# A cross-attention kernel: x added to the output by an adding transfer, a tile of its own for the returning values, and new orders of the work

## The chip, the cores and the metric

The kernel runs on one core of one Trainium2 chip. The core has TensorE (PE in the profile, with its weight loads as PEld), VectorE (DVE), ScalarE (ACT), GpSimd (POOL) and SyncE (SP), on-chip memory (SBUF), eight banks of accumulator memory in front of TensorE (PSUM) and 16 DMA engines. The metric is the device time of one execution in microseconds (us); the time before is the median of three executions. All times below are microseconds unless ns is written.

## The reference

For each of 32 batches there are x and y (the context), both 256 channels by 1024 positions in float32. What is computed, cut to what matters:

```python
x_q = einsum('oc,bcn->bno', w_qk, y)
x_k = einsum('oc,bcn->bon', w_qk, x)
x_v = einsum('oc,bcn->bon', w_v, x) + b_v
energy = einsum('bnc,bcm->bnm', x_q, x_k)              # 1024 x 1024 a batch
attention = softmax(energy, axis=-1)
attention = attention / (1e-07 + attention.sum(axis=1, keepdims=True))
x_r = einsum('bcn,bnm->bcm', x_v, attention)
out = x + relu(einsum('oc,bcn->bon', w_t, x - x_r) + b_t)
```

## The kernel before

**What TensorE multiplies.** A number in float32 is carried as forms of TensorE's faster type: a rounded high form, a rest form (what the rounding lost) and a low form (the high one scaled down by 4096, plus the rest). Each product is then three products with the three forms. The weights are prepared once: gw (w_qk with itself, so that keys of x meet raw y), vw (w_t with w_v, so that the values already carry the last projection) and tw (w_t). After that, each batch is 22 blocks of 12 matrix products, of 512 columns each:

- k0, k1: keys (`keys`, line 431), gw with x's forms; the result becomes gf's three forms by one ScalarE and two VectorE instructions.
- v0, v1: values (`values`, line 436), one for each half of the positions. They come out with channels on partitions and are needed with positions there: VectorE transposes 32 x 32 blocks into `turned`, four transfers on SP's queue put that into the DRAM tile `blocks`, and one more transfer brings it back in the new order. The first half comes back into the tile `yr`, the second into `turned`. ScalarE and GpSimd make uf's forms of it. In the tokens below the first half is v0 for the next batch (computed ahead), the second V1 in its own batch.
- W0, W1: w_t times x (`straight`, line 486), put into `xe` by ScalarE.
- E0 to E7: energies of 128 positions (`energy`, line 494), gf with y's forms yf. Then VectorE takes the minimum of each row, ScalarE the exponential with the row's sum, VectorE the reciprocal; VectorE adds the normalized rows to the column sums (`acc`), ScalarE makes ef's high form, VectorE its rest form, both on halves of 512 columns, ScalarE the scaled high form and GpSimd adds the rest to it.
- A0 to A7: attention times values (`attention`, line 549), ef with uf, summed in PSUM over the eight.

S are the column sums' last steps (`sums`, line 563) and O the finish of a batch (`finish`, line 589): for each half of the channels VectorE scales the attention's result into `z`, GpSimd adds xe, ScalarE takes the ReLU, SP's queue loads x again into the tile `xo`, GpSimd adds it, and SP's queue stores z to the output. X (`load_x`, line 372) loads the next batch's x and makes its three forms; Y2 and Y3 (`load_y`, line 340) do so for the two halves of the next batch's y. There the third form is -high by ScalarE, to which an adding transfer on GpSimd's queue adds y from DRAM; the low form is the scaled high, to which a second adding transfer, waiting for the first, adds the third. The first piece of the first half of batch 0 is done by GpSimd instead.

**PSUM.** The eight banks are four pairs. Pairs 2 and 3 take the attention's sums, and before A0 also the blocks marked ^ in the tokens (`high_pair`); pairs 0 and 1 take all other blocks in turn (`next_pair`). A block must wait until the pair's last user has been read.

**What sets the order.** The program first lists all operations: SET_UP, then for each batch the tokens of FIRST (batch 0), STEADY (batches 1 to 29), BEFORE (batch 30) or LAST (lines 167 to 181). TensorE's order is that of the tokens. For the other queues (VectorE, ScalarE, GpSimd, SP) the class `Plan` plays the list through with a price for each operation (lines 240 to 267: columns by a rate, plus a constant, plus a lag; a landing time for each transfer) and takes, on each engine, the ready operation that is due first. The due times are worked out from the end. What comes out is one fixed order for each queue, tied by the class `InOrder` (line 221); its call is line 231, so nearly every instruction in the profile bears L231, and groups are told apart by their tiles. On the chip each queue runs in that order and waits at an instruction whose input is not there.

## Time and profile before

| | |
|---|---|
| median of three executions | 1881.93 us (1878.26 to 1883.33) |
| the profiled execution: time, span from first to last instruction | 1882.61 us, 1880.7 us |
| granted TensorE clock, mean | 0.998 |
| busy: PE, DVE, ACT, POOL | 99%, 79%, 79%, 82% |
| DMA: bytes, mean rate | 301.88 MB, 161 GB/s |
| DMA queues, share of the 16 engines: hardware (SP's), software (GpSimd's) | 34.4%, 31.0% |

A row of a timeline holds the start and the time taken, the engine, the line, the operation, what it writes and reads, how many instructions were merged, and in brackets how long the engine had been idle before it and what ended that. A row of a group holds the total busy time, the mean of one in ns, and the idle time before the group's instructions. A row of a window holds its ends and length, then busy time and count for PE, PEld, DVE, ACT and POOL, the granted clock, the share of time that the DMA engines were busy and their rate. A row of waits names who waited for whom: total, times, longest. A row of a transfer ends with its size and the median time from issue to landing. Matrix products overlap, so a block's length is read from the start of one block to the start of the next.

### The profile page before, as it was taken

How to read it: one execution, taken by the hardware profiler on the slowest of the kernel's cores; microseconds unless marked ns; L12 is line 12 of the kernel's file. 1: busy time of each engine (PE TensorE's matmuls, PEld its weight loads, DVE VectorE, ACT ScalarE, POOL GpSimd, SP SyncE). 2: the span in 40 equal slices, each digit the busy share in tenths (PEclk: the TensorE clock that was granted, in tenths of full speed). 3: DMA queues.
4: the chain of work that ended last, by engine and by line, in shares of the span. 5: the costliest groups of instructions: out<-in, count | busy, mean ns of one | idle time of the engine just before them, and what ended most of it. 6: DMA issues, size and time to landing. Idle time of an engine off the chain costs nothing.

```text
span 1880.7 us, 24352 instructions
## 1 busy us (share of the span) xinstructions
PE 1855.6 (99%) x8494; PEld 1597.4 (85%) x8494; DVE 1493.0 (79%) x2106; ACT 1484.8 (79%) x1936; POOL 1541.4 (82%) x773
## 2 busy tenths in 40 slices
PE   8999999999999999999999999999999999999998
PEld 7888888888888888888888888888888888888887
DVE  6787777887778878878777787777887877877878
ACT  6788777897777987778877789777797777887775
POOL 4788888888788888788888888888888788888777
PEclk9999999999999999999999999999999999999999
DMA  6666766667667667666676666666767666667652
GB/s 187 137 154 169 178 157 157 162 163 178 160 154 170 154 183 173 152 153 162 167 180 157 157 160 165 175 160 152 174 152 184 169 154 151 170 165 177 150 119 79
DMA packets 128651, 301.88 MB, mean 161 GB/s; under 512 B 12688, under 2 KB 47120, under 8 KB 128528
## 3 DMA queue, kind: packets, MB, share of 16 engines
q1 hardware_dynamic: 92272, 200.45, 34.4%
q0 software_dynamic: 35680, 99.10, 31.0%
q8 instruction: 66, 1.08, 0.2%
q10 hardware_dynamic: 576, 0.79, 0.1%
q14 instruction: 57, 0.47, 0.1%
HBM read 167.38 MB, written 67.11 MB: 125 GB/s over the span
## 4 chain that ended last, share of the span: by engine, by line
PE 33%; ACT 28%; DVE 14%; DMA 11%; issue 8%; POOL 4%; SPq 1%; DVEq 0%; POOLq 0%; ACTq 0%
PE banks L231 33%; ACT ef L231 10%; DMA blocks<-turned 6%; ACT banks L231 5%; DVE ef L231 5%; ACT xf L231 5%; DMA yr<-blocks 4%; DVE acc L231 4%; ACT xe L231 3%; ACT uf L231 3%; POOL ef L231 2%; DVE small L231 2%; ACT z L231 1%; SPq L231 1%; DVE parts L231 1%
## 5 line engine op out<-in xcount | busy, mean ns | idle before, releaser
L231 PE MATMUL banks<-gf,yf 128*128 128x512 f32 x3072 | 705.5, 381 | 8.5 <-DMA yf<-yf 2.8
L231 POOL TENSOR_TENSOR ef<-ef 128x1024 fp32r<-128x1024 f32 x256 | 640.5, 2516 | 79.8 <-DVE acc L231 35.4
L231 PE MATMUL banks<-ef,uf 128*128 128x512 f32 x3072 | 694.7, 379 | 1.1 <-POOL ef L231 0.6
L231 PEld LDWEIGHTS banks<-gf,yf 128*128 128x128 f32 x3072 | 576.2, 189 | 107.5 <-DVE ef L231 24.9
L231 PEld LDWEIGHTS banks<-ef,uf 128*128 128x128 f32 x3072 | 580.2, 189 | 85.1 <-POOL ef L231 1.4
L231 DVE TENSOR_REDUCE small<-banks 128x1 f32<-128x1024 f32 x256 | 312.5, 1221 | 174.1 <-PE banks L231 174.1
L231 DVE SCALAR_TENSOR_TENSOR ef<-banks,small,ef 128x512 fp32r<-128x512 f32 x512 | 366.5, 742 | 48.5 <-ACT ef L231 47.6
L231 ACT ACTIVATE ef<-banks,small 128x512 fp32r<-128x512 f32 x512 | 335.5, 706 | 4.1 <-DVE acc L231 0.6
L231 DVE SCALAR_TENSOR_TENSOR acc<-banks,small,acc 128x512 f32<-128x512 f32 x448 | 319.6, 743 | 5.7
L231 ACT ACTIVATE banks<-banks,small 128x1024 f32<-128x1024 f32 x256 | 281.8, 1101 | 23.2 <-DVE small L231 23.0
L231 ACT ACTIVATE ef<-ef 128x1024 fp32r<-128x1024 f32 x256 | 276.7, 1081 | 1.2
L231 ACT ACTIVATE gf<-banks 128x1024 fp32r<-128x1024 f32 x64 | 65.4, 1023 | 261.7 <-PE banks L231 259.8
L231 POOL TENSOR_TENSOR z<-z,xe 128x1024 f32<-128x1024 f32 (+1 forms) x64 | 149.1, 2345 | 68.2 <-DVE z L231 65.7
L231 POOL TENSOR_TENSOR uf<-yr,uf 128x1024 fp32r<-128x1024 f32 x64 | 152.2, 2377 | 57.4 <-ACT uf L231 57.1
L231 PE MATMUL banks<-xf,vw 128*128 128x512 f32 x768 | 183.4, 383 | 7.5 <-DVE ef L231 6.7
L231 PE MATMUL banks<-xf,gw 128*128 128x512 f32 x768 | 177.3, 380 | 1.1 <-DVE xf L231 0.7
L231 PE MATMUL banks<-xf,tw 128*128 128x512 f32 x774 | 176.5, 378 | 0.9 <-DVE banks L231 0.9
L231 PEld LDWEIGHTS banks<-xf,vw 128*128 128x128 f32 x768 | 142.6, 189 | 38.2 <-DVE ef L231 19.2
L231 PEld LDWEIGHTS banks<-xf,gw 128*128 128x128 f32 x768 | 144.7, 189 | 23.5 <-ACT acc L231 1.1
L231 PEld LDWEIGHTS banks<-xf,tw 128*128 128x128 f32 x774 | 145.4, 189 | 22.1 <-DVE banks L231 1.3
L231 POOL TENSOR_TENSOR uf<-turned,uf 128x1024 fp32r<-128x1024 f32 x64 | 154.9, 2420 | 8.5 <-ACT uf L231 6.2
L231 POOL TENSOR_TENSOR xf<-xr,xf 128x1024 fp32r<-128x1024 f32 x62 | 149.3, 2429 | 1.0 <-ACT xf L231 1.0
(68 smaller groups left out, 1633.8 us busy)
## 6 DMA issues: line engine op xcount, KB each, us to landing
yr<-in_ctx_dram SPq DMA_DIRECT2D x64, 512.0 KB, 4.3
blocks<-turned SPq DMA_DIRECT2D x256, 128.0 KB, 3.2
yf<-in_ctx_dram POOLq DMA_DIRECT2D x63, 512.0 KB, 6.1
yf<-yf POOLq DMA_DIRECT2D x63, 512.0 KB, 7.4
xo<-in_x_dram SPq DMA_DIRECT2D x62, 512.0 KB, 4.4
xr<-in_x_dram SPq DMA_DIRECT2D x62, 512.0 KB, 4.8
xf<-xf POOLq DMA_DIRECT2D x62, 512.0 KB, 6.7
out_dram<-z SPq DMA_DIRECT2D x62, 512.0 KB, 4.1
```

Of the source, the lines that this page charges most:

```text
L231: self.last = getattr(self.engine, name)(*args, **kwargs)
```

## The change

- `finish`: the load of x into `xo` and GpSimd's addition go; in their place an adding transfer on GpSimd's queue adds x from DRAM to z after the ReLU. The tile `xo` goes.
- `load_y`: for all pieces but the first of all, the third form is now y minus the high form, by GpSimd from `yr`; ScalarE's -high and the adding transfer from DRAM go. The second adding transfer (third to low) stays.
- `values`: the first half comes back to a new tile `vb` and no longer to `yr`.
- `energy`: the column sums and the high and rest forms are written as three functions that can each work on halves or on the whole; SUMS, HIGHS and RESTS are 2, halves as before. They are listed sums, high forms, rest forms, and no longer half by half.
- All five token strings are new, and so are several of the planner's prices and landing times.

```diff
+SUMS, HIGHS, RESTS = 2, 2, 2
+LAND_Y, LAND_X, LAND_BLOCKS, LAND_BACK, LAND_LOW, LAND_Z = 7.6, 5.6, 3.4, 3.5, 7.0, 7.1
 SET_UP = (
-    "z z x0 z z z z G H fH00 x1 fH01 T fR01 fL00 y fR00 fL01 Q fR11 fH10 fR10 fL10 b fH11 fL11"
+    "z G z z z z x0 z fH00 y T fR01 fH01 x1 H fL01 Q fL00 fR10 fH10 fR00 fL10 fL11 b fR11 fH11"
 )
 FIRST = (
-    "V0^ W0^ W1^ E0 E1^ V1^ E2 E3 A0 A1 E4 X Y2 E5 A2 A3 E6 E7 A4 Y3 A5 v0 k0 S A6 A7 k1 O"
+    "V0^ W0^ E0 W1^ E1^ E2 V1^ E3 X A0 E4 Y2 A1 E5 A2 A3 E6 E7 A4 A5 k1 v0 Y3 A6 S A7 O k0"
 )
 STEADY = (
-    "W0^ E0^ E1 E2 W1^ V1^ E3 Y2 A0 E4 A1 E5 A2 X E6 A3 E7 Y3 S A4 A5 v0 k1 A6 A7 k0 O"
+    "W0 E0^ E1 E2 V1^ W1^ E3 A0 E4 A1 E5 X A2 A3 E6 E7 A4 A5 Y2 k0 v0 A6 S A7 O k1 Y3"
 )
 BEFORE = (
-    "V1^ E0 W0^ E1 W1^ X E2 A0 E3 A1 E4 A2 E5 A3 E6 E7 Y2 A4 Y3 A5 v0 k0 k1 A6 S A7 O"
+    "V1^ E0 W0 E1^ W1^ E2 E3 X A0 A1 E4 A2 E5 A3 E6 E7 A4 A5 Y2 Y3 v0 k1 A6 k0 S A7 O"
 )
 LAST = (
-    "E0 E1^ V1^ E2 E3 A0 A1 E4 E5 A2 A3 E6 R1 E7 A4 A5 W0 A6 a0 S a1 D1 F1 G0"
+    "E0 R1 E1^ V1^ E2 E3 A0 A1 E4 A2 E5 A3 E6 E7 A4 A5 W0 A6 S a0 a1 D1 F1 G0"
 )
...
-        plan.add("act", columns / 1200 + 0.1 + more, 0.09, reads, writes, trace)
+        plan.add("act", columns / 1200 + 0.13 + more, 0.1, reads, writes, trace)
...
-        plan.add("dve", columns / 960 + 0.16, 0.0, reads, writes, trace, early=early)
+        busy = columns / 960 + (0.08 if columns > MB else 0.13)
+        plan.add("dve", busy, 0.08, reads, writes, trace, early=early)
...
-        busy = columns * 2.25 / 1024 + 0.12
-        plan.add("pool", busy, 0.0, reads, writes, trace, port=busy)
+        busy = columns * 2.25 / 1024 + 0.07
+        plan.add("pool", busy, 0.08, reads, writes, trace, port=busy)
...
-    xo = one.tile([P, N], F32, name="xo")
+    vb = one.tile([P, N], F32, name="vb")
...
-            on_act(columns, nh, nr, lambda: act.mul(third, value(high), -1.0))
-            by_pool(7.2, nr, nr, lambda: accumulate(third, from_[:, :, at]))
+            on_pool(
+                columns, ["yr"] + nh, nr,
+                lambda: pool.tensor_tensor(third, r[:, :, at], value(high), ALU.subtract),
+            )
...
-        plan.add("sync", 2.4, 3.0 if b else 5.0, ["turned"], ["blocks"], out_of)
-        back, name = (turned, "turned") if q else (flat(yr), "yr")
-        by_sync(4.5, ["blocks"], [name], lambda: sync.dma_start(back, blocks))
+        plan.add("sync", 1.75, LAND_BLOCKS if b else 5.0, ["turned"], ["blocks"], out_of)
+        back, name = (turned, "turned") if q else (vb, "vb")
+        by_sync(LAND_BACK, ["blocks"], [name], lambda: sync.dma_start(back, blocks))
...
-        for h in range(MH):
-            halves(h)
+        each, whole = [[h] for h in range(MH)], [list(range(MH))]
+        for make, pieces in ((column_sums, SUMS), (high_form, HIGHS), (rest_form, RESTS)):
+            for hs in each if pieces == MH else whole:
+                make(hs)
...
-                by_sync(5.2, ["bias"], ["xo"], lambda: sync.dma_start(xo, x[b, ts(c, P)]))
-                on_pool(
-                    N, [f"z{c}", "xo"], [f"z{c}"],
-                    lambda: pool.tensor_tensor(z[:, c], z[:, c], xo, ALU.add),
-                )
+                by_pool(LAND_Z, [f"z{c}"], [f"z{c}"], lambda: accumulate(z[:, c], x[b, ts(c, P)]))
```

The other landing times become LAND_Y (y, 5.8 before), LAND_X (x, 5.0), LAND_LOW (the transfers into low forms, 5.8 for y and 8.2 for x).

More of the change, by code (lines that the diff above doesn't have):

```diff
@@ L376, in of @@
                 raw = [f"xr{k}{h}" for h in range(MH)]
[L377 to L378 removed]
+                by_sync(LAND_X, ["yr"] if b == 1 else [], raw, lambda: sync.dma_start(xr[:, k], x[b, ts(k, P)]))
+                on_act(
+                    N, raw, x_names(HIGH, k), lambda: act.copy(parted(xf[:, HIGH, k]), in_turn(xr[:, k])), more=0.47
+                )
                 on_pool(
@@ L517, in energy, with part @@
             N, at + [nm[0]], at + [nm[1]],
-            lambda: act.activation(p, p, AF.Exp, bias=low, scale=-1.0, accum_out=rs), more=0.193,
+            lambda: act.activation(p, p, AF.Exp, bias=low, scale=-1.0, accum_out=rs), more=0.1,
         )
         dve_small(0.18, [nm[1]], [nm[2]], lambda: dve.reciprocal(ri, rs))
-        def halves(h):
-            ph, a, turns = both[:, h], acc[:, ts(h, MB)], in_turn(both[:, h])
-            to = {j: parted_half(f[:, j], h) for j in (HIGH, REST)}
-            high, rest = names[HIGH][h], names[REST][h]
+        def part(t, hs):
+            return t[:, hs[0] * MB : (hs[-1] + 1) * MB]
@@ L526, in halves, with column_sums @@
+        def column_sums(hs):
+            ph, a = part(p, hs), part(acc, hs)
+            banks_, sums_ = [at[h] for h in hs], [f"acc{h}" for h in hs]
             if n == 0:
-                on_dve(MB, [at[h], nm[2]], [f"acc{h}"], lambda: dve.tensor_scalar(a, ph, ri, None, ALU.mult))
+                on_dve(
+                    MB * len(hs), banks_ + [nm[2]], sums_,
+                    lambda: dve.tensor_scalar(a, ph, ri, None, ALU.mult),
+                )
             else:
                 on_dve(
-                    MB, [at[h], nm[2], f"acc{h}"], [f"acc{h}"],
+                    MB * len(hs), banks_ + [nm[2]] + sums_, sums_,
@@ L531, in halves, with turned_to, high_form @@
                     lambda: dve.scalar_tensor_tensor(a, ph, ri, a, ALU.mult, ALU.add),
                 )
-            on_act(MB, [at[h], nm[2]], [high], lambda: act.mul(to[HIGH], turns, ri))
+        def turned_to(j, hs):
+            return parted(f[:, j])[:, :, hs[0] * MB // 2 : (hs[-1] + 1) * MB // 2]
+        def high_form(hs):
+            turns = in_turn(part(p, hs))
+            on_act(
+                MB * len(hs), [at[h] for h in hs] + [nm[2]], [names[HIGH][h] for h in hs],
+                lambda: act.mul(turned_to(HIGH, hs), turns, ri),
+            )
@@ L534, in halves, with rest_form @@
+        def rest_form(hs):
+            turns = in_turn(part(p, hs))
             on_dve(
-                MB, [at[h], nm[2], high], [rest],
+                MB * len(hs), [at[h] for h in hs] + [nm[2]] + [names[HIGH][h] for h in hs],
+                [names[REST][h] for h in hs],
                 lambda: dve.scalar_tensor_tensor(
-                    to[REST], turns, ri, value(to[HIGH]), ALU.mult, ALU.subtract
+                    turned_to(REST, hs), turns, ri, value(turned_to(HIGH, hs)), ALU.mult, ALU.subtract
```

10 lines of the change are left out of this document (4 added, 6 removed).

## The prediction

> **What bounds the kernel now.** The page's first part comes first: TensorE (PE) is busy 99%, the others 79 to 82%.
>
> ```profile
> PE 1855.6 (99%) x8494; PEld 1597.4 (85%) x8494; DVE 1493.0 (79%) x2106; ACT 1484.8 (79%) x1936; POOL 1541.4 (82%) x773
> ```
>
> So only time in which PE waits can be won. The timeline of PE shows where. One batch, from its E0 to the next:
>
> ```profile
> 899.46 7.93 PE L231 MATMUL banks<-gf,yf 128*128 128x512 f32 x36
> 907.23 2.75 PE L231 MATMUL banks<-xf,tw 128*128 128x512 f32 x12
> 909.82 1.46 PE L231 MATMUL banks<-xf,vw 128*128 128x512 f32 x6
> 911.94 1.56 PE L231 MATMUL banks<-xf,vw 128*128 128x512 f32 x6 [0.66 <-DVE ef L231]
> ...
> 918.54 3.15 PE L231 MATMUL banks<-gf,yf 128*128 128x512 f32 x12
> 921.53 2.75 PE L231 MATMUL banks<-ef,uf 128*128 128x512 f32 x12
> ...
> 944.84 2.75 PE L231 MATMUL banks<-xf,gw 128*128 128x512 f32 x12
> ...
> 957.79 4.48 PE L231 MATMUL banks<-gf,yf 128*128 128x512 f32 x20
> ```
>
> Read the starts. A block of 12 products takes 907.23 to 909.82, 2.59 us, and a batch has 22 blocks, 56.98 us. This batch takes 957.79 - 899.46 = 58.33, so it lost 1.35: 0.93 in the middle of V1 (six products there took 2.12 in place of 1.30), some 0.4 in E4 (918.54 to 921.53 is 2.99), and little else. Over the 27 periods from the third batch's E0 to the thirtieth's, the stage's window and its waits say:
>
> ```profile
> 147.48:1708.89 1561.41, 1553.22 (x7130) 1340.44 (x7128) 1248.27 (x1756) 1249.42 (x1620) 1305.12 (x649) 1.00 0.68 164
> ...
> ACT uf L231 <- DMA yr<-blocks: 62.8, 27, 3.5
> ```
>
> 1561.41 - 27 x 56.98 = 22.9 us lost, 0.85 a period, at a full clock. ScalarE waits 2.3 us in each period for the values' return from DRAM. That return decides the loss, as three batches show (E0's start, the cast that ends the wait for the return, the next E0; for the middle one 899.46 and 957.79 stand above):
>
> ```profile
> 87.43 7.93 PE L231 MATMUL banks<-gf,yf 128*128 128x512 f32 x36
> 92.00 1.05 ACT L231 CAST uf<-yr 128x1024 fp32r<-128x1024 f32 x1 [2.31 <-DMA yr<-blocks]
> 147.48 7.93 PE L231 MATMUL banks<-gf,yf 128*128 128x512 f32 x36
> ...
> 901.93 1.05 ACT L231 CAST uf<-yr 128x1024 fp32r<-128x1024 f32 x1 [2.90 <-DMA yr<-blocks]
> 904.84 1.08 ACT L231 ACTIVATE banks<-banks,small 128x1024 f32<-128x1024 f32 x1
> ...
> 959.23 1.04 ACT L231 CAST uf<-yr 128x1024 fp32r<-128x1024 f32 x1 [1.87 <-DMA yr<-blocks]
> 1015.35 4.91 PE L231 MATMUL banks<-gf,yf 128*128 128x512 f32 x22
> ```
>
> Return after E0's start: 4.57, 2.47, 1.44 us. Lost in that period: 3.07 (60.05), 1.35, 0.58 (57.56). So 0.8 us is lost for each us that the return is later. The way: E0's exponential (904.84) stands behind the cast in ScalarE's queue, E0's forms come late, and V1 waits for E0's bank.
>
> The opening has its own loss:
>
> ```profile
> 17.87 2.75 PE L231 MATMUL banks<-xf,vw 128*128 128x512 f32 x12
> ...
> 33.41 1.03 PE L231 MATMUL banks<-gf,yf 128*128 128x512 f32 x4
> 37.27 6.27 PE L231 MATMUL banks<-gf,yf 128*128 128x512 f32 x20 [2.84 <-DMA yf<-yf]
> 43.38 5.34 PE L231 MATMUL banks<-ef,uf 128*128 128x512 f32 x24
> ...
> 37.20:41.50 4.30, 4.23 (x12) 3.40 (x13) 2.92 (x4) 2.70 (x3) 3.13 (x2) 0.60 1.00 214
> ```
>
> E2 and E3 of batch 0 took 9.97 for 5.18: 3.0 idle for y's adding transfer, and then 1.8 because the clock was granted at 0.60. From 17.87 to 87.43 lie 24 blocks, 62.2 us, in 69.56: 7.4 lost, 4.8 of it here.
>
> By the Trainium skill ("TensorE: Matmul & The Clock Gate", HAM oscillation) the clock halves after gaps over some 3.4 us; here some 3.0 were enough. By that rule or by the row, the 1.8 go as soon as this gap is shorter; the sum below has them gone in either case.
>
> **The change, part by part.** These groups and transfers carry the costs:
>
> ```profile
> L231 POOL TENSOR_TENSOR z<-z,xo 128x1024 f32<-128x1024 f32 x62 | 147.1, 2373 | 0.0
> L231 ACT ACTIVATE yf<-yf 128x1024 fp32r<-128x1024 f32 x126 | 140.1, 1112 | 0.0
> L231 POOL DMA_DIRECT2D yf<-in_ctx_dram x64 | 78.6, 1234 | 30.3 <-DVE ef L231 25.7 <-ACT yf L231 4.6
> ...
> yf<-in_ctx_dram POOLq DMA_DIRECT2D x63, 512.0 KB, 6.1
> yf<-yf POOLq DMA_DIRECT2D x63, 512.0 KB, 7.4
> ```
>
> *x added by a transfer.* 62 GpSimd adds (147 us) and 62 loads on SP's queue go, and 62 adding transfers come. Nothing shows their price; the nearest is y's adding transfer from DRAM, 1.23 us on GpSimd and 6.1 to land. The output leaves some 4 us later, and nobody waits: z is written again a batch later. GpSimd now stands at such a transfer until the ReLU is done, with uf's and the first ef's sums behind it; at worst that delays A0.
>
> *y's third form on GpSimd.* 63 multiplications go from ScalarE (63 x 1.112 = 70 us, 2.2 a batch), and 64 transfers from GpSimd (79); 63 subtractions come, of the removed add's size (2.37, together 149). GpSimd: -147 + 76 - 79 + 149 = -1 us of 1541. That is no gain and no loss; ScalarE alone is relieved, and y waits for one landing where it waited for two.
>
> *Sums and forms in new functions.* With the three settings at 2 they are the same instructions on the same halves: nothing.
>
> *A tile of its own (vb), the orders, the planner's prices.* SP's queue and yr are freed. In the new order v0 is followed by A6, A7, k1, W0 and then E0: four blocks, 10.36 us, where it had five. How long the return takes:
>
> ```profile
> 945.94 1.25 DVE L231 STREAM_TRANSPOSE turned<-banks 128x1024 f32<-128x1024 f32 x1
> 947.22 2.44 SPq L231 DMA_DIRECT2D blocks<-turned  x4
> 955.57 0.34 SPq L231 DMA_DIRECT2D yr<-blocks  x1
> ...
> 915.89 1.77 SPq L231 DMA_DIRECT2D blocks<-turned  x4
> 920.62 0.34 SPq L231 DMA_DIRECT2D turned<-blocks  x1
> ...
> 915.90:920.60 4.70, 4.57 (x21) 3.69 (x21) 3.30 (x5) 4.70 (x6) 4.70 (x3) 1.00 0.49 123
> 947.20:955.60 8.40, 8.40 (x40) 7.37 (x39) 6.04 (x5) 1.23 (x2) 4.06 (x4) 1.00 1.05 215
> ```
>
> v0 ended at 944.84. The transpose came 1.10 later, behind the column sums' small steps, which now have 2.6 us more to be over (I take 0.2). Then 1.28 to the first piece's issue, 8.35 to the return's issue while the DMA engines are full (1.05), against 4.73 for v1 where they are half free (0.49), and 3.66 to the cast. In the new order the cast comes 0.2 + 1.28 + L + 3.66 - 10.36 = L - 5.22 after E0's start. L lies between 4.73 and 8.35. Two of the four y transfers of a batch are gone beside it and x's two adding ones start later, so I take the middle, 6.54: 1.3 us after E0's start. By the line above that loses 0.55 a period in place of 0.85: 27 x 0.3 = **-8.0**. Ends: L of 4.73 and E4's wait gone too, -22.9; L of 8.35, +3.1 us, 1.9 a period, +28. That W1 and V1 change places alters no distance: W1 now waits for E0's bank three blocks after it.
>
> *Set-up.* G's products are put ahead of five of the ten fillers.
>
> ```profile
> 1.06 4.63 PE L231 MATMUL banks<-few 128*128 128x128 f32 x20 [1.06 <-DVE few L231]
> 5.48 2.63 PE L231 MATMUL banks<-z 128*128 128x256 f32 x8
> ```
>
> Half of the fillers are 2.2 us, so G can start by up to that much earlier, if its weights are there; but two more steps (4 products, 0.86) now follow the last low piece, which VectorE makes late. Between -2.2 and +0.9; I take less than the middle, as the weights' landing is not told: **-0.4**.
>
> *Batch 0.* The second piece's third form is one subtraction now, not a transfer.
>
> ```profile
> 19.30 1.72 POOL L231 TENSOR_TENSOR yf<-yf 128x512 fp32r<-128x512 f32 x1
> 24.18 1.22 DVE L231 SCALAR_TENSOR_TENSOR gf<-banks,gf 128x1024 fp32r<-128x1024 f32 x1
> 26.37 1.69 POOL L231 DMA_DIRECT2D yf<-yf  x1
> ```
>
> GpSimd is free at 21.0, a half subtraction later (1.2) the low transfer starts at some 22.3 instead of 26.37, and lands after 7.4 (its row) or 10.9 (37.27 - 26.37): 29.7 to 33.2. E2 now comes after five blocks, at 30.4, and needs it 0.9 later: 0 to 1.9 lost. E0 moves up to 22.7 (two blocks after 17.5) and needs gf's last form, ready at 25.4, or 24.2 if the values' transpose gives way, from 24.4 on: 0 to 1.0 lost. Together some 1.3, against 4.8. But PE then reaches the rest earlier than ScalarE and VectorE have moved, so part comes back: **-3.5**, ends -7.4 and +1. The first steady period falls from 3.07 to some 1.2: **-1.9** (-3.1 to +1).
>
> *The end.* From 1708.89 on I can price no wait of the new order: **-0.5**, ends -4 and +3.
>
> The sum is -0.4 - 3.5 - 1.9 - 8.0 - 0.5 = -14.3. The profiled execution took 1882.6 (span 1880.7), 0.7 above the median of 1881.93: 1868.3, and about **1868** as a median.
>
> **The rivals.** Told from no change here is 0.3%, 5.6 us: 1876.3 to 1887.6.
>
> 1. *Only the opening gains.* The return comes as late as before, the steady loss stays 0.85. For it: one block less of distance. Against: less traffic, a freer ScalarE. 1882.6 - 6.3 = 1876.
> 2. *The return comes later (slower).* The blocks land as slowly as now (L 8.35), as the four-block distance is not made good; x's adding transfers crowd the way back. 1882.6 - 6.3 + 28 = 1905; it decides from a return 2.1 us after E0's start on, where the opening's gain is eaten. For it: the full DMA engines in the window. Against: two transfers fewer in it, and xe and the ReLU can run ahead of the late cast.
>
>    The Trainium skill ("DMA: Bandwidth & Descriptors", Issuing engines are not separate DMA queues) speaks for this rival: transfers from all queues run on the same 16 engines and interleave, so moving x's to GpSimd's queue frees none. The two windows agree.
> 3. *Nearly all waits go.* The return comes before E0 (L below 5.2) and E4's bank is in time: 1882.6 - 22.9 - 6.3 = 1853.
> 4. *Nothing moves.* What the opening wins, ScalarE and VectorE give back in batch 0, and the orders trade one wait for another: 1882.
>
> **How the numbers follow.** The forecast 0.45, rivals 0.18, 0.17, 0.12, 0.08. Low 1850 takes in the third. High 1892 is the second with L of 7.7 (2.5 after E0, 1.43 a period, +15.7 with the opening's -6.3); what lies above is some one in ten. Faster: most of the forecast, half of the first rival, the third: 0.64. Slower: nearly all of the second and a little of the fourth: 0.18. Same: 0.18.
>
> **What would show it.** Right: E0-to-E0 periods of 57.4 to 57.6; the cast from vb within 1.5 us of E0's start; no half clock after 30 us; ScalarE 70 us less busy, GpSimd within 20 of 1541. Wrong: periods of 58 and over with ScalarE waiting over 2.5 us for vb; PE waiting for POOL's ef before A0, which would mean that GpSimd stands at x's transfer; a new wait at k0 or v0, which now follow E6 and E7 by three blocks each; or a wait for y in E2 longer than 2 us.

## The result, and the profile after

| | before | after |
|---|---|---|
| median of four executions each | 1880.1 us (1877.52 to 1883.33) | 1847.99 us (1847.77 to 1848.07) |
| ratio after / before, 95% interval | | 0.9828 (0.981 to 0.9846) |
| span of the profiled execution | 1880.7 us | 1846.1 us |
| bytes moved | 301.88 MB | 268.58 MB |

The change made the kernel 1.7% faster, more than twice the 13.6 us that were forecast, and 2 us below the low end of the range. The instructions of the kernel after bear L233, since two lines were added above the call.

The first and the fourth part of the page of the kernel after (busy time by engine; the chain that ended last, by engine):

```profile
PE 1835.8 (99%) x8494; PEld 1603.5 (87%) x8494; DVE 1478.3 (80%) x2106; ACT 1462.4 (79%) x1872; POOL 1523.1 (83%) x773
...
PE 95%; DVE 2%; DMA 2%; SPq 0%; issue 0%; ACT 0%; POOL 0%; DVEq 0%; ACTq 0%
```

PE's share reads 99% as before, and says nothing of the gain. The chain does: PE now makes 95% of it. In the kernel before, the same row gave PE 33%, ACT 28%, DVE 14% and DMA 11%, so the path went in and out of TensorE all the time. Now the end of the program hangs on TensorE alone, nearly everywhere.

One steady batch of the kernel after, in PE's timeline, up to A1 (the next E0 starts at 993.18):

```profile
936.21 7.93 PE L233 MATMUL banks<-gf,yf 128*128 128x512 f32 x36
943.98 2.75 PE L233 MATMUL banks<-xf,vw 128*128 128x512 f32 x12
946.57 2.75 PE L233 MATMUL banks<-xf,tw 128*128 128x512 f32 x12
949.15 2.75 PE L233 MATMUL banks<-gf,yf 128*128 128x512 f32 x12
951.74 2.75 PE L233 MATMUL banks<-ef,uf 128*128 128x512 f32 x12
954.33 2.75 PE L233 MATMUL banks<-gf,yf 128*128 128x512 f32 x12
956.92 2.75 PE L233 MATMUL banks<-ef,uf 128*128 128x512 f32 x12
```

Every start is 2.59 behind the last one: V1 runs through (before, 0.93 was lost in its middle), and E4 to A1 is 2.59 (before, 2.99). The period is 56.97, the bare 22 blocks. The window over the same 27 periods as in the prediction, and ScalarE's row among the waits:

```profile
138.21:1677.08 1538.87, 1538.87 (x7129) 1346.93 (x7128) 1235.29 (x1756) 1233.00 (x1566) 1288.33 (x649) 1.00 0.59 148
```

```profile
ACT uf L233 <- DMA vb<-blocks: 1.9, 2, 1.0
```

1538.87 - 27 x 56.98 = 0.41 us lost, against 22.95. ScalarE waited for the return twice in the whole run. SP's and ScalarE's timelines around one return (batch with E0 at 1107.15) show how early it is:

```profile
1098.89 1.79 SPq L233 DMA_DIRECT2D blocks<-turned  x4
1102.59 0.34 SPq L233 DMA_DIRECT2D vb<-blocks  x1
```

```profile
1108.36 1.03 ACT L233 CAST uf<-vb 128x1024 fp32r<-128x1024 f32 x1
1111.19 1.09 ACT L233 ACTIVATE banks<-banks,small 128x1024 f32<-128x1024 f32 x1 [0.85 <-DVE small L233]
```

The way through DRAM (first transfer of the blocks to the issue of the return, L in the prediction) took 3.70, where 8.35 was read before and 6.54 was forecast. The cast from vb has no wait in brackets: it starts 1.21 after E0, as in all steady batches, because xe's instruction stands ahead of it in ScalarE's queue. E0's exponential now waits for VectorE's minimum of the row, not for the cast.

The opening of the kernel after, in PE's timeline (16.62 is the first product of the values):

```profile
16.62 2.75 PE L233 MATMUL banks<-xf,vw 128*128 128x512 f32 x12
...
21.92 3.21 PE L233 MATMUL banks<-gf,yf 128*128 128x512 f32 x12
24.96 2.75 PE L233 MATMUL banks<-xf,tw 128*128 128x512 f32 x12
...
37.91 0.46 PE L233 MATMUL banks<-ef,uf 128*128 128x512 f32 x1
39.56 2.88 PE L233 MATMUL banks<-ef,uf 128*128 128x512 f32 x11 [1.19 <-DVE ef L233]
42.28 2.86 PE L233 MATMUL banks<-gf,yf 128*128 128x512 f32 x12
```

The wait for y's adding transfer is gone. What is left is 0.45 in E0 (24.96 - 21.92 = 3.04 for 2.59) and 1.78 in A0 (42.28 - 37.91 = 4.37), whose first ef comes late. The granted clock from 16.62 to the next batch's E0 at 81.23 is 1.00. So the 34.5 us of the two spans divide thus:

| stretch | lost before | lost after | gain | forecast |
|---|---|---|---|---|
| set-up, to the values' first product | 17.87 | 16.62 | 1.25 | 0.4 |
| batch 0 | 7.41 | 2.45 | 4.96 | 3.5 |
| first steady period | 3.07 | 0.00 | 3.07 | 1.9 |
| 27 steady periods | 22.95 | 0.41 | 22.54 | 8.0 |
| last three batches, and what follows the last product | 10.1 | 7.4 | 2.7 | 0.5 |

(The set-up's two entries are times, not losses.) Two thirds of the gain, and 14.5 of the 20.2 us that the forecast missed, lie in the steady periods. There the experiments were made.

### The profile page after: what moved, and what is told of

Its sections match the earlier page's. It is cut to its first block, busy times and chain, and to the rows that moved or that the text cites. A ratio compares the mean times of both kernels' runs of the same rounds, so it can differ in the third digit from the quotient of the medians.

```text
span 1846.1 us, 24208 instructions
## 1 busy us (share of the span) xinstructions
PE 1835.8 (99%) x8494; PEld 1603.5 (87%) x8494; DVE 1478.3 (80%) x2106; ACT 1462.4 (79%) x1872; POOL 1523.1 (83%) x773
## 2 busy tenths in 40 slices
DMA packets 111242, 268.58 MB, mean 145 GB/s; under 512 B 11664, under 2 KB 45840, under 8 KB 111120
## 3 DMA queue, kind: packets, MB, share of 16 engines
q8 instruction: 66, 1.08, 0.2%
## 4 chain that ended last, share of the span: by engine, by line
PE 95%; DVE 2%; DMA 2%; SPq 0%; issue 0%; ACT 0%; POOL 0%; DVEq 0%; ACTq 0%
PE banks L233 95%; DMA blocks<-turned 1%; DMA vb<-blocks 1%; DVE ef L233 0%; DVE acc L233 0%; SPq L233 0%; DMA z<-in_L_xattn_w_t_dram 0%; DVE small L233 0%; DMA turned<-blocks 0%; DVE parts L233 0%; DVE turned L233 0%; DVE z L233 0%; DVE rc L233 0%; POOL uf L233 0%; ACT banks L233 0%
## 5 line engine op out<-in xcount | busy, mean ns | idle before, releaser
L233 POOL TENSOR_TENSOR ef<-ef 128x1024 fp32r<-128x1024 f32 x256 | 624.4, 2460 | 93.2 <-ACT ef L233 64.9
L233 PE MATMUL banks<-gf,yf 128*128 128x512 f32 x3072 | 691.0, 379 | 1.7 <-DVE ef L233 1.6
L233 PE MATMUL banks<-ef,uf 128*128 128x512 f32 x3072 | 690.1, 379 | 1.2 <-DVE ef L233 1.2
L233 PEld LDWEIGHTS banks<-gf,yf 128*128 128x128 f32 x3072 | 579.8, 189 | 86.7 <-DVE ef L233 3.7
L233 PEld LDWEIGHTS banks<-ef,uf 128*128 128x128 f32 x3072 | 580.2, 189 | 85.0 <-DVE ef L233 1.9
L233 DVE TENSOR_REDUCE small<-banks 128x1 f32<-128x1024 f32 x256 | 312.5, 1221 | 155.7 <-PE banks L233 155.6
L233 DVE SCALAR_TENSOR_TENSOR ef<-banks,small,ef 128x512 fp32r<-128x512 f32 x512 | 371.6, 743 | 46.0 <-ACT ef L233 45.3
L233 ACT ACTIVATE ef<-banks,small 128x512 fp32r<-128x512 f32 x512 | 333.6, 685 | 48.7 <-DVE acc L233 44.7
L233 DVE SCALAR_TENSOR_TENSOR acc<-banks,small,acc 128x512 f32<-128x512 f32 x448 | 323.0, 746 | 5.8
L233 ACT ACTIVATE banks<-banks,small 128x1024 f32<-128x1024 f32 x256 | 278.7, 1089 | 52.1 <-DVE small L233 49.5
L233 ACT ACTIVATE ef<-ef 128x1024 fp32r<-128x1024 f32 x256 | 267.8, 1060 | 4.1
L233 POOL TENSOR_TENSOR z<-z,xe 128x1024 f32<-128x1024 f32 (+1 forms) x64 | 158.1, 2473 | 98.2 <-DVE z L233 96.6
L233 ACT ACTIVATE gf<-banks 128x1024 fp32r<-128x1024 f32 x64 | 65.4, 1023 | 217.7 <-PE banks L233 217.6
L233 POOL TENSOR_TENSOR xf<-xr,xf 128x1024 fp32r<-128x1024 f32 x62 | 150.3, 2424 | 73.9 <-ACT xf L233 73.9
L233 POOL TENSOR_TENSOR uf<-vb,uf 128x1024 fp32r<-128x1024 f32 x64 | 156.1, 2439 | 30.3 <-ACT uf L233 30.3
L233 PE MATMUL banks<-xf,tw 128*128 128x512 f32 x774 | 176.3, 378 | 1.1 <-DVE banks L233 1.1
L233 PE MATMUL banks<-xf,gw 128*128 128x512 f32 x768 | 177.1, 380 | 0.0
L233 PE MATMUL banks<-xf,vw 128*128 128x512 f32 x768 | 176.2, 379 | 0.0
L233 POOL TENSOR_TENSOR yf<-yr,yf 128x1024 fp32r<-128x1024 f32 (+1 forms) x65 | 164.2, 2527 | 5.4 <-ACT yf L233 5.4
L233 PEld LDWEIGHTS banks<-xf,tw 128*128 128x128 f32 x774 | 145.4, 189 | 21.9 <-DVE banks L233 1.5
L233 PEld LDWEIGHTS banks<-xf,vw 128*128 128x128 f32 x768 | 145.2, 189 | 20.6
L233 PEld LDWEIGHTS banks<-xf,gw 128*128 128x128 f32 x768 | 145.0, 189 | 20.5
```

Source lines behind the costliest of these rows:

```text
L233: self.last = getattr(self.engine, name)(*args, **kwargs)
```

## The experiments

**How they are read.** Each kernel's steady loss is the time from the third batch's E0 to the thirtieth's, less 27 x 56.98, from its own trace. The ratio is to runs of the kernel before on the same chip. The ratio's interval reaches 0.1 to 0.5% to either side, so a difference of a few us between two rows rests on the steady loss, not on the ratio. The rows come from several chips, so close medians are compared by their ratios.

| kernel | median us | ratio (95%) | steady loss, a period |
|---|---|---|---|
| before | 1880 | 1 | 0.85 |
| work of after, orders and prices of before | 1871.41 | 0.9964 (0.9948 to 0.998) | 0.62 |
| orders and prices of after, work of before | 2372.42 | 1.2623 (1.257 to 1.2675) | 17.6 |
| before, with only y's subtraction on GpSimd | 1872.61 | 0.996 (0.9944 to 0.9975) | 0.72 |
| after, y's third form by transfer as before | 2082.25 | 1.1079 (1.102 to 1.1137) | 7.4 |
| after, first half back to yr | 2174.67 | 1.1571 (1.1527 to 1.1614) | 11.0 |
| after, x added by GpSimd | 1846.68 | 0.9825 (0.9796 to 0.9853) | 0.00 |
| after, tokens of before | 1855.37 | 0.9871 (0.9842 to 0.99) | 0.15 |
| after, prices of before | 1867.83 | 0.9933 (0.9911 to 0.9956) | 0.31 |
| work of after + VectorE's prices | 1866.57 | 0.9915 (0.9882 to 0.9948) | 0.58 |
| work of after + GpSimd's prices, landing times | 1872.27 | 0.9942 (0.9918 to 0.9967) | 0.76 |
| work of after + ScalarE's prices | 1859.33 | 0.9877 (0.9841 to 0.9912) | 0.15 |
| work of after + price of the cast of x | 1859.81 | 0.9887 (0.9844 to 0.9929) | 0.26 |
| work of after + ScalarE's other prices | 1860.22 | 0.9889 (0.9845 to 0.9933) | 0.31 |
| before + price of the cast of x | 1875.86 | 0.9974 (0.9963 to 0.9985) | 0.60 |
| after, STEADY's tokens for batch 30 | 1848.08 | 0.9817 (0.9782 to 0.9851) | 0.015 |
| after, x added by GpSimd, STEADY's tokens for batch 30 | 1847.55 | 0.9821 (0.9779 to 0.9863) | 0.01 |
| after | 1847.99 | 0.9828 (0.981 to 0.9846) | 0.015 |

### Work and orders apart

The first question was whether the steady gain comes from the instructions and transfers of the change (its "work") or from its orders, that is its token strings and prices.

The work alone: after, with the five token strings and all prices of before.

```diff
 STEADY = (
-    "W0 E0^ E1 E2 V1^ W1^ E3 A0 E4 A1 E5 X A2 A3 E6 E7 A4 A5 Y2 k0 v0 A6 S A7 O k1 Y3"
+    "W0^ E0^ E1 E2 W1^ V1^ E3 Y2 A0 E4 A1 E5 A2 X E6 A3 E7 Y3 S A4 A5 v0 k1 A6 A7 k0 O"
...
-        plan.add("act", columns / 1200 + 0.13 + more, 0.1, reads, writes, trace)
+        plan.add("act", columns / 1200 + 0.1 + more, 0.09, reads, writes, trace)
```

> The work of after (x by an adding transfer, y's third form on GpSimd, vb) with the token strings and the planner's prices and landing times of before. Traffic theory: the return is issued some 4 us after the first blocks transfer, ScalarE waits for it less than 0.3 a period, V1's wait of some 0.45 a period goes and only E4's 0.4 stays; 1862 to 1870. Order theory: the loss stays at 0.7 to 0.9 a period, 1876 to 1882.

Orders and prices alone: after, with y's third form, the return to yr and x's addition as before.

```diff
-        back, name = (turned, "turned") if q else (vb, "vb")
+        back, name = (turned, "turned") if q else (flat(yr), "yr")
...
-                by_pool(LAND_Z, [f"z{c}"], [f"z{c}"], lambda: accumulate(z[:, c], x[b, ts(c, P)]))
+                by_sync(5.2, ["bias"], ["xo"], lambda: sync.dma_start(xo, x[b, ts(c, P)]))
```

> The work of before (x added by GpSimd from xo, y's third form by ScalarE and a transfer from DRAM, the values back in yr) with the token strings and the planner's prices of after. Traffic theory (the steady loss hangs on how late the values' return is, and that on y's transfers from DRAM beside it): the return is issued 6 to 8 us after the first blocks transfer, and the steady loss stays at 0.6 to 1.5 us a period; 1870 to 1900. Order theory (the orders and prices alone take the waits away): at most 0.2 a period, 1850 to 1860.

The orders alone are 26% slower. The waits of that kernel:

```profile
PE banks L233 <- DMA yf<-in_ctx_dram: 250.6, 30, 9.1
...
PE banks L233 <- DMA yf<-yf: 112.1, 30, 5.1
```

The new strings put Y2 and Y3 late in the batch, shortly before the y they make is needed. With two adding transfers behind each other TensorE then waits up to 9.1 us, and the granted clock is 0.90 on the mean. The tile yr, which y and the returning values share here as before, has a part in it: in one batch (return issued at 971.70) y's next load into yr is issued only 11.0 later. Neither theory had this. So the orders can only be had with the new work.

The work alone gains 0.4% and keeps 0.62 of the 0.85; its 1871.41 lies between the two theories. SP's and PE's timelines of one batch of it:

```profile
939.35 1.79 SPq L233 DMA_DIRECT2D blocks<-turned  x4
944.58 0.34 SPq L233 DMA_DIRECT2D vb<-blocks  x1
```

```profile
949.73 7.93 PE L233 MATMUL banks<-gf,yf 128*128 128x512 f32 x36
...
960.09 2.91 PE L233 MATMUL banks<-xf,vw 128*128 128x512 f32 x12
962.84 2.77 PE L233 MATMUL banks<-gf,yf 128*128 128x512 f32 x12
...
968.04 3.15 PE L233 MATMUL banks<-gf,yf 128*128 128x512 f32 x12
971.02 2.75 PE L233 MATMUL banks<-ef,uf 128*128 128x512 f32 x12
```

The return is issued 5.15 ahead of E0, and nothing waits for it. Still V1 takes 2.75 from start to start and E4 2.98: 0.16 and 0.39, together with 0.02 in E3 the 0.58 that nearly every batch of this kernel loses. In this kernel, too, the cast starts 1.21 after E0, the earliest that xe ahead of it allows. So the prediction's third batch, with its cast at 1.44, stood at the foot of the line, and the 0.58 that it lost is the same 0.58.

The trace of before says so too, if all of its 27 steady batches are read and not three. None loses less than 0.58. Six lose 0.58 or 0.59, with casts from 1.04 to 1.67 after E0 (a seventh, at 1.66, loses the same in V1, E3 and E4, and 0.20 more in A2 and E6). From there the loss rises about one for one: 0.76 at 1.89, 0.93 at 2.05, 1.35 at 2.48, 1.93 at 3.05. The slope of 0.8 was a chord across this bend. Of the 22.95 us, 27 x 0.58 = 15.7 are there however early the return comes, and 7.3 come with its lateness. **The 0.58 was never the return's.**

### The parts of the work

Before, with nothing but y's subtraction:

```diff
-            on_act(columns, nh, nr, lambda: act.mul(third, value(high), -1.0))
-            by_pool(7.2, nr, nr, lambda: accumulate(third, from_[:, :, at]))
+            on_pool(
+                columns, ["yr"] + nh, nr,
+                lambda: pool.tensor_tensor(third, r[:, :, at], value(high), ALU.subtract),
+            )
```

> Before with one edit: y's third form is y minus the high form by GpSimd (no multiplication on ScalarE, no transfer of y from DRAM). Traffic theory: this part alone brings the return forward: 4 to 5.5 us from the first blocks transfer to the return's issue (8.35 before), ScalarE's wait for yr from 2.3 a period to under 0.5, the loss from 0.85 to 0.6 a period, the opening 3 us better; 1868 to 1874. If the own tile or x's transfer is what matters: 0.8 to 0.9 a period, 1876 to 1882. As GpSimd gets 73 us more to do here (86% busy), a third way is that it holds up ef's sums: over 1882.

The steady loss falls to 0.72, and the opening gains most: the third batch's E0 comes at 139.44 (147.48 before, 138.22 after). SP's timeline and the waits:

```profile
936.62 1.78 SPq L231 DMA_DIRECT2D blocks<-turned  x4
944.13 0.34 SPq L231 DMA_DIRECT2D yr<-blocks  x1
```

```profile
ACT uf L231 <- DMA yr<-blocks: 8.1, 9, 4.0
```

The way through DRAM is still 7.51, so that y's two transfers fewer do not shorten it much by themselves; yet ScalarE's wait for it falls from 79.2 in the whole run to 8.1. The return is issued 0.8 earlier (3.1 ahead of E0 in the median batch, 2.3 in before), and xe's instruction, behind the cast in before, now stands ahead of it. The 0.72 is not the 0.85 less a piece: V1 loses 0.24, E4 nothing, and A1 and E5 0.21 and 0.25, where before lost nothing. No price was changed here; the new work alone made the planner order the queues anew. GpSimd is at 1605.8 us, 86%: the two additions of x and the two subtractions of y are all on it.

After, with y's third form by the transfer again (the diff above, reversed):

> After with y's forms as before alone (third form -high by ScalarE, y added to it by a transfer from DRAM). Traffic theory: 6 us or more from the first blocks transfer to the return's issue, ScalarE waits for vb, 0.3 to 1.5 lost a period, 1858 to 1890. Order theory: 0 to 0.1 a period, 1848 to 1852.

```profile
ACT uf L233 <- DMA vb<-blocks: 223.1, 32, 9.9
```

This is the second rival in its pure form, and it costs far more than the 0.3 to 1.5 a period that were expected. The return is issued some 10 us after the first blocks' transfer, 1.0 to 2.7 after E0's start, and its cast comes 5.3 to 11.2 after it. In two batches next to each other the cast came at 10.09 and 7.16 and the periods lost 8.6 and 6.8; the prediction's line gives 0.58 + 0.8 x (10.09 - 1.44) = 7.5, and 5.2. The loss lies 1.1 to 1.6 above that line. One for one from a cast at 1.7 on, as the batches of before have it, would give 9.0 and 6.0, one above and one below; half clock may have a part (0.956 granted on the mean). So a late return costs about its lateness, far outside the points that the line was drawn through.

After, with the first half back to yr:

```diff
-        back, name = (turned, "turned") if q else (vb, "vb")
+        back, name = (turned, "turned") if q else (flat(yr), "yr")
```

> After, but the values' first half comes back to yr as before, which y's halves pass through too. Both theories: nothing in the steady stage unless yr's next load of y or the return has to wait for the other: 1848 to 1852. If the own tile is what brings the return forward, the return's issue moves 2 us or more back and 0.3 or more is lost a period: 1858 or more.

The waits, and SP's timeline:

```profile
PE banks L233 <- DMA yf<-yf: 229.6, 29, 9.5
```

```profile
958.15 0.34 SPq L233 DMA_DIRECT2D yr<-blocks  x1
969.95 0.40 SPq L233 DMA_DIRECT2D yr<-in_ctx_dram  x1
```

Here the return itself is early. But v0 stands between Y2 and Y3 in the new string, so Y3's load of y needs the tile that the return fills and ScalarE has yet to read: it is issued 11.8 later, and E's y is late by up to 9.5. The tile of its own is therefore the condition of the new order; in this order it is worth 2174.67 - 1847.99 = 327 us. The text above expected such a loss from a later return only.

After, with x loaded into a tile that is free by then (rc), and added by GpSimd; both halves are scaled first:

```diff
+            scaled()
+        for c in range(KC):
...
-                by_pool(LAND_Z, [f"z{c}"], [f"z{c}"], lambda: accumulate(z[:, c], x[b, ts(c, P)]))
+                by_sync(4.4, ["bias"], ["rc"], lambda: sync.dma_start(rc, x[b, ts(c, P)]))
+                on_pool(
+                    N, [f"z{c}", "rc"], [f"z{c}"],
+                    lambda: pool.tensor_tensor(z[:, c], z[:, c], rc, ALU.add),
+                )
```

> After, but x is added as before, by a load on SP's queue and GpSimd's addition; the copy stands in the tile rc, which is free once both halves are scaled (a tile xo beside vb has no room). GpSimd gets some 80 us more (87% busy). If x's adding transfer is only a matter of room: 0 to 0.1 a period, 1848 to 1852. If it is what keeps GpSimd in time: PE waits for ef's sums or uf, 0.2 to 1.5 a period, 1854 to 1890.

The first part of its page:

```profile
PE 1834.8 (99%) x8494; PEld 1603.0 (87%) x8494; DVE 1477.8 (80%) x2106; ACT 1463.3 (79%) x1872; POOL 1611.4 (87%) x773
```

GpSimd has 88 us more to do, the steady loss is nil, and the ratio is that of after (0.9825 and 0.9828). So the adding transfer of x, the first thing that the change names, is worth no time here. What it gives is room: it needs neither xo nor another tile. That xo would not fit beside vb, as the text above says, no run shows.

The Trainium skill ("DMA: Bandwidth & Descriptors", Issuing engines are not separate DMA queues) says that transfers run on the same 16 DMA engines whichever engine issued them. This pair agrees: the DMA engines are busy 0.59 of the steady window with x on GpSimd's queue and 0.55 with x on SP's.

### Tokens and prices

After, with the five strings of before (one is shown), all new prices kept:

```diff
-    "W0 E0^ E1 E2 V1^ W1^ E3 A0 E4 A1 E5 X A2 A3 E6 E7 A4 A5 Y2 k0 v0 A6 S A7 O k1 Y3"
+    "W0^ E0^ E1 E2 W1^ V1^ E3 Y2 A0 E4 A1 E5 A2 X E6 A3 E7 Y3 S A4 A5 v0 k1 A6 A7 k0 O"
```

> After with the five token strings of before; work and prices are after's. The work of after in the orders of before loses 0.58 a period: 0.2 in V1, 0.39 in E4, at places where VectorE's queue has the wrong step first. Token theory (V1 ahead of W1 and the new places of X, Y, k, v free VectorE in time): 0.4 to 0.6 stays, 1864 to 1871. Price theory (the planner's new prices put VectorE's steps in the right order, whatever the tokens): at most 0.2 a period, 1850 to 1860, the opening's loss being that of the old tokens (some 4 to 7).

After, with the prices and landing times of before (the core), new strings kept:

```diff
-LAND_Y, LAND_X, LAND_BLOCKS, LAND_BACK, LAND_LOW, LAND_Z = 7.6, 5.6, 3.4, 3.5, 7.0, 7.1
+LAND_Y, LAND_X, LAND_BLOCKS, LAND_BACK, LAND_LOW, LAND_Z = 5.8, 5.0, 3.0, 4.5, 5.8, 7.1
...
-        plan.add("act", columns / 1200 + 0.13 + more, 0.1, reads, writes, trace)
+        plan.add("act", columns / 1200 + 0.1 + more, 0.09, reads, writes, trace)
...
+        plan.add("dve", columns / 960 + 0.16, 0.0, reads, writes, trace, early=early)
```

> After with the planner's prices and landing times of before; work and tokens are after's. Token theory: at most 0.2 a period, 1848 to 1856. Price theory: 0.4 to 0.9 a period, 1860 to 1875.

Either alone leaves a little of the steady loss, 0.15 and 0.31, where neither (the work alone) leaves 0.62. With the new prices 20 of the 27 batches lose nothing and seven lose 0.3 to 1.0; with the new strings nearly each loses 0.26. The first is what the price theory asked for; the second's loss lies between the two theories. So strings and prices do much the same job in the steady batches, and each goes half of the way or more. VectorE's timeline behind E0 shows what the job is. The work alone (E0 at 949.73), then after (E0 at 936.21):

```profile
958.18 0.75 DVE L233 SCALAR_TENSOR_TENSOR ef<-banks,small,ef 128x512 fp32r<-128x512 f32 x1 [0.27 <-ACT ef L233]
...
959.51 1.21 DVE L233 TENSOR_REDUCE small<-banks 128x1 f32<-128x1024 f32 x1
960.64 0.74 DVE L233 SCALAR_TENSOR_TENSOR ef<-banks,small,ef 128x512 fp32r<-128x512 f32 x1
```

```profile
944.74 0.75 DVE L233 SCALAR_TENSOR_TENSOR ef<-banks,small,ef 128x512 fp32r<-128x512 f32 x1 [0.35 <-ACT ef L233]
...
946.07 0.74 DVE L233 SCALAR_TENSOR_TENSOR ef<-banks,small,ef 128x512 fp32r<-128x512 f32 x1
...
948.04 1.22 DVE L233 TENSOR_REDUCE small<-banks 128x1 f32<-128x1024 f32 x1
```

In the first, E2's minimum (TENSOR_REDUCE) stands ahead of E0's second rest form, the last reader of E0's second bank. That form ends 11.65 after E0's start. The fourth block behind E0 (there V1, in after W1) writes to this bank from its seventh product on, at 4 x 2.59 + 1.30 = 11.66; there is no time left for the hand-over, and V1 waits. In the second the form comes first and ends 10.60 after E0's start; the minimum follows, with nothing waiting for it. No run exchanged these two instructions alone, but all traces agree. In the seven other kernels in which the minimum stands ahead of this form (before among them), the fourth block loses 0.16 or more in nearly every batch; in the eight in which it stands behind, hardly ever anything. Two are left. In after with y's transfer the late return covers all of it. In after with the prices of before the minimum has moved back by one form only, ahead of E1's two rest forms, and it is E3, the next user of E1's bank, that starts 0.16 late.

E4's loss has its place in ScalarE's queue. The work alone:

```profile
964.60 0.69 ACT L233 ACTIVATE ef<-banks,small 128x512 fp32r<-128x512 f32 x1
965.17 3.02 ACT L233 CAST xf<-xr 128x1024 fp32r<-128x1024 f32 x2
968.10 0.68 ACT L233 ACTIVATE ef<-banks,small 128x512 fp32r<-128x512 f32 x1
```

Both casts of the next batch's x, 1.5 each, stand between the two high forms of E2; the second comes 3.5 behind the first, E2's bank is read late, and E4 waits 0.39 for it. In before and in the kernel with VectorE's prices the two casts stand there in every steady batch, and E4 loses 0.40; of the kernels with one cast or none there, only the two whose E4 waits for y and the last one of the next section lose time in E4 in every batch.

### Which price

The next three kernels each add new prices to the work alone: VectorE's; GpSimd's with the landing times and SP's; ScalarE's.

```diff
+        busy = columns / 960 + (0.08 if columns > MB else 0.13)
+        plan.add("dve", busy, 0.08, reads, writes, trace, early=early)
```

> The work of after in the token strings of before, all prices of before but VectorE's, which are after's (a shorter busy time and a lag of 0.08). The work of after with all old prices loses 0.58 a period, with all new ones some 0.15 (27 periods: 4.0). VectorE theory (the wrong place of E2's minimum ahead of E0's second rest form comes from VectorE's own price): at most 0.25 a period, 1856 to 1862. If ScalarE's or the landing times' price puts it there: 0.4 to 0.7, 1866 to 1874.

```diff
+        busy = columns * 2.25 / 1024 + 0.07
+        plan.add("pool", busy, 0.08, reads, writes, trace, port=busy)
...
+LAND_Y, LAND_X, LAND_BLOCKS, LAND_BACK, LAND_LOW, LAND_Z = 7.6, 5.6, 3.4, 3.5, 7.0, 7.1
...
+        plan.add("sync", 1.75, LAND_BLOCKS if b else 5.0, ["turned"], ["blocks"], out_of)
```

> As the former, but only GpSimd's prices and the landing times are after's. Both VectorE's and ScalarE's theory: 0.5 to 0.7 a period stays, as the place of E2's minimum hangs on neither: 1866 to 1874. If the landing times matter: at most 0.3 a period, 1856 to 1864.

```diff
+        plan.add("act", columns / 1200 + 0.13 + more, 0.1, reads, writes, trace)
...
+                    N, raw, x_names(HIGH, k), lambda: act.copy(parted(xf[:, HIGH, k]), in_turn(xr[:, k])), more=0.47
...
+            lambda: act.activation(p, p, AF.Exp, bias=low, scale=-1.0, accum_out=rs), more=0.1,
```

> As the former, but only ScalarE's prices are after's. ScalarE theory: at most 0.25 a period, 1856 to 1862. VectorE theory: 0.4 to 0.7 a period, 1866 to 1874.

VectorE's prices leave both waits as they were (0.58 a period, 0.16 in V1 and 0.40 in E4). GpSimd's prices and the landing times do not leave them, though the sum hides it: E4's wait goes, V1's grows to 0.65, and ScalarE waits for the return again (51.2 in the whole run), which neither theory had. ScalarE's bring the loss to 0.15, in other places (E7 and A4). In that kernel (E0 at 945.88) VectorE's order is that of after:

```profile
955.74 0.74 DVE L233 SCALAR_TENSOR_TENSOR ef<-banks,small,ef 128x512 fp32r<-128x512 f32 x1
957.72 1.22 DVE L233 TENSOR_REDUCE small<-banks 128x1 f32<-128x1024 f32 x1
```

So prices of ScalarE decide the order of VectorE, presumably by the moment at which the planner believes that an input is there. Of ScalarE's prices the largest error was that of the cast of x, which reads its input in turn: some 1.5 us in the traces, 0.95 by the old price. Hence the last three runs: this price alone, the others without it, and this price in the kernel before.

```diff
+                    N, raw, x_names(HIGH, k), lambda: act.copy(parted(xf[:, HIGH, k]), in_turn(xr[:, k])), more=0.47
```

> The work of after in the tokens and prices of before, with one price changed: the cast of x in its woven order on ScalarE, planned at 0.95 and taking 1.55 in the trace, gets 0.47 more. All old prices lose 0.58 a period (0.2 in V1, 0.39 in E4), ScalarE's new prices together 0.15. Cast theory (two casts planned too short stand ahead of E2's second high form, so E4 waits for its bank): E4's 0.39 goes, 0.15 to 0.3 a period stays, 1857 to 1864. If the constant of all ScalarE operations or the exponential's price does it: 0.5 to 0.7, 1866 to 1873.

ScalarE's other prices (the diff before, without that line):

> The complement: all of ScalarE's new prices but that of the cast of x (0.13 in place of 0.1 for each operation, the exponential 0.1 in place of 0.193 more). Cast theory: E4's 0.39 stays, V1's 0.2 may go: 0.35 to 0.6 a period, 1863 to 1871. Other theory: at most 0.25, 1857 to 1862.

The cast's price alone, in the kernel before:

> Before with that one price (0.47 more for the cast of x) and nothing else. Cast theory: E4's 0.39 goes from the 0.85 a period, V1's, which hangs on the return, stays: 0.4 to 0.6, 1868 to 1875. If the return decides alone: 0.8 to 0.9, 1877 to 1883.

With the cast's price alone E4's wait goes and V1's stays (0.24); ScalarE's timeline has one cast ahead of the high form and one behind it:

```profile
959.92 1.52 ACT L233 CAST xf<-xr 128x1024 fp32r<-128x1024 f32 x1
961.35 0.69 ACT L233 ACTIVATE ef<-banks,small 128x512 fp32r<-128x512 f32 x1
963.02 1.58 ACT L233 CAST xf<-xr 128x1024 fp32r<-128x1024 f32 x1
```

But without it, by ScalarE's other prices, E4's wait goes as well and V1's stays (0.31 a period, between the two theories); GpSimd's prices did it too, and so did y's subtraction with no price changed. In the kernel before, the price of the cast does another thing. The minimum moves behind E0's form, and V1 loses nothing; xe moves ahead of the cast, the way through DRAM takes 6.7 in the median batch in place of 8.2, and ScalarE's wait for the return falls to 13.7 in the whole run. E4's 0.40 stays, but from another pair: E3's minimum now stands ahead of E2's second rest form (912.92 and 914.05 in VectorE's timeline), which ends 0.23 after E4's seventh product was due. So the theory that this one price was at fault fell. With the work of after, each half of ScalarE's new prices removes E4's wait and only both together move the minimum. What is shown is the places in the queues; which price leads to them cannot be put down to one.

### The end, and a faster version

Batch 30 of after still loses 1.93. Its string keeps W0 behind E0; here it is given STEADY's:

```diff
-        for token in (FIRST if b == 0 else LAST if b == B - 1 else BEFORE if b == B - 2 else STEADY).split():
+        for token in (FIRST if b == 0 else LAST if b == B - 1 else STEADY if b == B - 2 else STEADY).split():
```

> After with STEADY's token string for batch 30 in place of BEFORE's. After loses 1.9 in batch 30, most of it ahead of E4, which follows A0 and A1 there and stands between them in STEADY. If the string is the cause: 0 to 0.5 there, 1846 to 1847. If the end is short of work for the engines behind TensorE, the loss moves into the last batch: 1848.

Batch 30 then loses nothing, but batch 0 loses 4.97 in place of 2.45 and the last 3.17 in place of 1.08: the planner works its due times out from the end, so a string at the end can reorder the queues of the opening. The time is the same (1846.64 and 1849.51). The same edit with x added by GpSimd:

> x added from a loaded copy in rc (which ran at 1846.7) and STEADY's string for batch 30. Batch 30 loses nothing and the opening stays at 2.5 to 3: 1845 to 1846. As STEADY's string in after moved the loss into the opening and the last batch, this may: 1846.5 to 1849.

1847.55, no gain on the 1846.68 without it. The lowest times are those of after with x added by GpSimd, 1846.51 and 1846.85, where after's lowest is 1847.77. With two executions, another chip and ratios of 0.9825 and 0.9828, that is a hint and no finding.

## Why the prediction was wrong

**What was right.** The direction; that only time in which PE waits can be won; each term's sign and their order in size. The second piece's third form by subtraction took the opening's wait away, and with it the half clock: 0.60 over 4.3 us before, 1.00 all through batch 0 after. In before with nothing but that subtraction, E2 and E3 of batch 0 take 5.32, where they took 9.97. (The Trainium skill's page "TensorE: Matmul & The Clock Gate", HAM oscillation, would have the clock halve only after longer gaps than the 1.19 left in A0; the trace agrees.) GpSimd came out 18 us lower, inside the 20 allowed: its subtraction cost 2.53 and x's transfer 1.04 of its time (2.37 and 1.23 were taken), and no steady batch lost time to it. k0, k1 and v0 wait for nothing.

**The step that failed** is "A tile of its own, the orders, the planner's prices". It let one mechanism, the return, stand for the whole steady loss, and read from three batches a line that ended at 0.58 for a return 1.44 late. That batch was already on the flat part, where an earlier return wins nothing; only the outer end of the range, L of 4.73 "and E4's wait gone too", had the 0.58 gone. The rest of the term was right in size, though by luck in one step: its own line gives 0.48 for a cast 1.3 after E0, and it took 0.55. The 8.0 that it forecast are the 7.3 that lateness cost; the 14.5 by which it was short are the floor of 27 x 0.58 = 15.7, which it left in place. The work alone shows it plainly: there nobody waits for the return, and 0.58 stays in nearly every batch.

What the 0.58 is could have been read in the profile before, in the batch with E0 at 899.46:

```profile
910.01 1.22 DVE L231 TENSOR_REDUCE small<-banks 128x1 f32<-128x1024 f32 x1
911.14 0.74 DVE L231 SCALAR_TENSOR_TENSOR ef<-banks,small,ef 128x512 fp32r<-128x512 f32 x1
```

```profile
915.67 3.02 ACT L231 CAST xf<-xr 128x1024 fp32r<-128x1024 f32 x2
918.60 0.69 ACT L231 ACTIVATE ef<-banks,small 128x512 fp32r<-128x512 f32 x1
```

Its V1 waited 0.66 for "DVE ef": VectorE's rest form, which ended 12.42 after E0's start, behind a minimum that was not urgent; E4 waited for E2's bank, which the high form behind the two casts of x still had to read. The prediction put V1's wait down to E0's exponential being late by the cast. That is only one half: the minimum takes 1.13 from start to start, and without it the form would have ended at 11.29, ahead of the 11.66 at which V1 needs the bank. By this estimate even that late return would have cost V1 nothing. For the part that no return changes, the runs put V1's share on the place in VectorE's queue, and E4's on the casts of x. An order written by a planner is itself a resource; the prediction priced prices and strings at nothing beyond the return's distance.

**L was off too, but harmlessly.** 6.54 was taken between 4.73 and 8.35; it is 3.7 to 3.8 in 20 of the 27 batches (4.1 to 5.4 in the others), below the lower end. Of the parts, y's subtraction alone gave 7.5, the work 5.3, the whole 3.8 in the median batch, and the whole without the subtraction some 10. So it cannot be summed from parts. The work alone, with 5.3, was early enough already; the further 1.5 bought nothing. The sign that was named for the forecast, a cast within 1.5 of E0's start, was met with 1.21, and with it not the forecast's loss: the sign could not tell a return just in time from one that nobody waits for.

**The other terms.** The opening's three gave 9.3 for 5.8: batch 0 lost 2.45 (about 3.9 by the forecast), and the give-back that was feared in the first steady period did not come, its cast being at 1.21 as well. Set-up gave 1.25 for 0.4. The end gave 2.7 for 0.5, which had been left as unpriced.

**ScalarE's 70.** The page shows it 22 us less busy, and the step's cost was none the less right: the group of y's scaled forms fell from 141.7 to 68.2 us. The page's busy time counts overlapping records once: ScalarE's records overlapped by 212.7 us in all before and by 131.1 after.

**The rivals.** The third, nearly all waits go, is what happened, and by its two conditions: L below 5.2, and E4's bank in time. It gave 1853 and was given a chance of 0.12, as nothing in the forecast's reasoning could bring E4 in. Measured was 5 lower, the excess of the opening and of the end. The second rival's mechanism exists (the kernel with y's transfer kept), but it took two transfers more per batch to bring it on.

By ratio, the 1.7% come in this order: the work 0.4, ScalarE's prices to 1.2, all prices to 1.3, the strings to 1.7. The intervals of the first two steps lie apart, the others overlap; by the steady losses, 0.62, 0.15, 0.15 and 0.015 a period, the step from ScalarE's prices to all prices gave nothing, and the strings took the rest. The shares hang on the order: with the strings put ahead of the prices, work and strings give 0.7 and the prices the other 1.0.

**What stays open.** Which of ScalarE's prices moves the minimum, beyond that all of them do and neither half; what a kernel would do in which only the two places were exchanged by hand; and why the way through DRAM, with the work of after, is 3.8 with the new strings and prices, 4.2 to 4.3 with either alone and 5.3 with neither (medians).

## What to carry to other kernels

Draw the line of loss against lateness through all batches, and look for where it goes flat: what a batch with no lateness loses has another cause, and here it was 27 x 0.58 = 15.7 of the 34.5 us. Where a static plan orders the queues, follow the wait to the instruction that stands ahead of the awaited one on its engine, and ask whether anything needs it there; wrong prices cost nothing themselves, but the order that follows from them does. Parts of such a change are not terms of a sum: a new order without its free tile or its shorter chain cost 200 to 500 us, where all together gained 32.

## What was not expected of the hardware

Transfers landed sooner: the windows of the steady periods give the DMA engines as busy 0.59 of the time, 0.68 before. The page's medians from issue to landing, after:

```profile
blocks<-turned SPq DMA_DIRECT2D x256, 128.0 KB, 2.3
...
yf<-yf POOLq DMA_DIRECT2D x63, 512.0 KB, 4.7
...
z<-in_x_dram POOLq DMA_DIRECT2D x62, 512.0 KB, 7.3
```

The blocks took 3.2 before and the adding transfer within SBUF 7.4, with 12% more bytes in all. Fewer bytes are not the reason by themselves. Before with the price of the cast of x moves the 301.88 MB of before, and its blocks land in 2.5; before with y's subtraction moves the 268.58 MB of after, and they take 4.3. What lies beside a transfer in time may have a part; no run here separates it. The adding transfer of x from DRAM takes 7.3, above y's 6.1 that stood for it. Four executions of after agree within 0.3 us, where those of before lie up to 5.8 apart. Slack of the return is not all of that: the kernel with ScalarE's prices alone has it, and its executions still lie 3 apart (1857.81 to 1860.86).
